# Block exchange through HBM with one store and one load of all partitions

## The chip, the cores and the metric

The kernel runs on one core of a Trainium2 chip. The metric is the device time of one execution in microseconds (us); lower is better. The core has a matrix engine (TensorE, PE in the profile), VectorE (DVE), ScalarE (ACT), GpSimd (POOL) and SyncE (SP), which here only issues DMA transfers. On-chip memory (SBUF) and the matrix engine's accumulators (PSUM) have 128 partitions; HBM is reached by DMA.

## The reference

A transformer block over 16 sequences of 256 tokens with 256 features: a layer norm with a shift from a conditioning vector, attention with 16 heads of 64 with normalised queries and keys, and a mixture of 8 experts in which every expert takes the 512 tokens with the largest gate. All of it is in 32-bit floating point.

```python
shift = silu(t) @ W_ada.T + b_ada
h = _ln(x, ln1_g, ln1_b) + shift
qkv = (h @ Wqkv.T).reshape(b, n, 3, H, HD)
q = _ln(qkv[:, :, 0].transpose(0, 2, 1, 3), qn_g, qn_b)
k = _ln(qkv[:, :, 1].transpose(0, 2, 1, 3), kn_g, kn_b)
v = qkv[:, :, 2].transpose(0, 2, 1, 3)
attn = softmax(einsum('bhnd,bhmd->bhnm', q, k) / sqrt(HD))
o = einsum('bhnm,bhmd->bhnd', attn, v)
x = x + o.transpose(0, 2, 1, 3).reshape(b, n, H * HD) @ Wout.T
tok = x.reshape(-1, d)
gate = softmax(tok @ Wgate.T)
vals, idx = top_k(gate.T, bs // E)
g = _ln(tok[idx], mlp_g, mlp_b)
y = gelu(g @ fc1s[e].T + b1s[e]) @ fc2s[e].T + b2s[e]     # for each expert e
out = tok.at[idx].add(y * vals)
```

## The kernel before

The program has a start-up (loads, centring of weights), an attention stage over the 16 sequences, a routing stage (which tokens go to which expert) and an expert stage of 16 jobs. Up to the first expert job the order of the instructions is written out by hand: every step is registered with `at(...)` (L1333 to L1517), and the list `PLACES` (L182 to L526) holds one number for each. `plan.order(PLACES)` (L1519) sorts by it, and the steps are issued in that order, so each engine and SP's DMA queue run their own steps strictly in this sequence. A step that must wait holds back all later ones of its engine.

**Queries and keys** (class `Group`). A group is 512 columns of the projection (8 heads of 64) for 128 tokens; groups 0 and 1 are the queries, 2 and 3 the keys, 4 and 5 the values, and t is the half of the sequence. TensorE multiplies (`matmul`, L688), ScalarE squares (L701), VectorE sums the squares of each head (`stats`, L705), GpSimd takes the power -1/2 (L711, L103), and VectorE multiplies each head by it (`scale`, L721). The means need no work there: the weight columns are centred once at the start, head by head (`center`, L604 and L605, eight calls, two for each group).

**The exchange.** The matrix engine needs features (and later keys) on the partitions, while they come out along the rows. Instead of transposing on TensorE, the kernel lets VectorE transpose blocks of 32x32 inside each band of 32 partitions (`turn`, L754 and L851). What is left is to bring block q of band k to band q. That goes through HBM. `away` (L761, L859) stores the 128 partitions of 4 KB each to a tile `blocks[k, m, q, 256]`, where k is the band, m the row in it and q the quarter, 1 KB each. The tile is made with five quarters, of which four are used, so the rows lie 5 KB apart. `back` (L773, L873) waits until the store has landed and issues four loads, one for each quarter q, of 32 partitions and four pieces of 1 KB each: row m of quarter q goes to partition 32q + m. Each sequence has four exchanges for queries and keys (tiles kb, kblocks, and qraw or kT) and eight for attention weights (pb, blocks, prT). All of them are issued on SP's queue, with the loads of x and the stores of tok and its norm. After the load, ScalarE applies gain and bias (`affine`, L781 for queries, L789 for keys).

The first and the last sequence (`DIRECT`, L171) do not use the exchange: TensorE transposes (L730, L881) and ScalarE copies out of PSUM (L742, L888).

**Attention** (class `Quad`, four heads). For a pair of heads (i), TensorE computes the scores into two PSUM tiles (`scores`, L813; there are four such tiles). VectorE takes the row maxima (L821), ScalarE the exponentials with their row sums (`exps`, L830), VectorE inverts the sums of both heads together (L837), GpSimd multiplies (L841), and VectorE turns the blocks (L851). The exchange brings the keys to the partitions, and TensorE multiplies with the values (`product`, L900), from where ScalarE copies to SBUF (L915). For the rows of the values to meet the right keys, the score columns are in the order (q, c, m): L806 reads the keys by quarter, so that column (q, c, m) is key 128c + 32q + m, and it lands on partition 32q + m.

**The rest of a sequence** (class `Tail`): the output projection (L926), the residual (L933), stores (L937, L947), and the gate's logits (L963).

Of the kernel before, what the change touches and what calls it, by code (L numbers as in the profile page):

```python
# [9 lines left out]
F32 = mybir.dt.float32  # L10
I32 = mybir.dt.int32
BF16 = mybir.dt.bfloat16
AF = mybir.ActivationFunctionType
ALU = mybir.AluOpType
AX = mybir.AxisListType
# [3 lines left out]
P = 128  # L19
B, N, D = 16, 256, 256  # L20
H, HD = 16, 64
# [5 lines left out]
TB = N // P  # L27
# [7 lines left out]
SQ = 32  # L35
QB = P // SQ
GW = 512
# [27 lines left out]
def kernel(  # L65
# [14 lines left out]
    nc = tc.nc  # L80

    const = ctx.enter_context(tc.tile_pool(name="const", bufs=1))
    dram = ctx.enter_context(tc.tile_pool(name="dram", bufs=1, space=DRAM))
# [87 lines left out]
    DIRECT = (0, B - 1)  # L171
# [356 lines left out]
    if True:  # L528
# [7 lines left out]
        wq = attw.tile([P, DC, 3 * H * HD], F32, name="wq")  # L536
        wo = attw.tile([P, HP, D], F32, name="wo")
        xs, hTs, qTs, kTs, vs, oTs = {}, {}, {}, {}, {}, {}
# [60 lines left out]

        def center(g, c):  # L600

            w3 = wq[:, c, bass.ts(g, GW)].rearrange("p (h d) -> p h d", d=HD)
            ws = stat.tile([P, 8], F32, tag="ws", bufs=2, name="ws")
            nc.vector.tensor_reduce(ws, w3, AX.X, ALU.add)  # L604
            nc.vector.scalar_tensor_tensor(  # L605
                w3, ws.unsqueeze(2).to_broadcast([P, 8, HD]), -1.0 / HD, w3, ALU.mult, ALU.add
            )

        class Norm:

# [21 lines left out]
        class First:  # L632
# [4 lines left out]
            def stats(self, t):  # L637
                self.norms[t] = Norm(xs[self.b][:, t, :], "l1")
# [34 lines left out]
        def plain(kT):  # L673
            return kT.rearrange("p g k t h m -> p (g k t h m)").rearrange("p (h n) -> p h n", n=N)

        class Group:
# [26 lines left out]
            def stats(self):  # L703
                self.ss = stat.tile([P, 2, 8], F32, tag="ss", name="ss")
                nc.vector.tensor_reduce(  # L705
                    self.ss[:, 0, :], self.sq.rearrange("p (h d) -> p h d", d=HD),
                    AX.X, ALU.add,
                )

            def power(self):  # L710
# [5 lines left out]
            def scale(self):  # L716
                engine, src = nc.gpsimd, self.qk
                if src is None:
                    self.qk = work.tile([P, GW], F32, tag="qk", bufs=3, name="qk")
                    engine, src = nc.vector, self.pm  # L720
                engine.tensor_tensor(  # L721
                    self.qk.rearrange("p (h d) -> p h d", d=HD),
                    src.rearrange("p (h d) -> p h d", d=HD),
                    self.ss[:, 1, :].unsqueeze(2).to_broadcast([P, 8, HD]), ALU.mult,
                )

            def transposes(self):
# [23 lines left out]
            def turn(self, kb):  # L751
                if self.t == 0:
                    kb.append(work.tile([P, QB, TB, HP // 2, SQ], F32, tag="pb", bufs=3, name="kb"))
                nc.vector.transpose(  # L754
                    kb[0][:, :, self.t],
                    self.qk.rearrange("p (h q d) -> p q h d", q=QB, d=SQ),
                )

            def away(self, kb):
                self.blocks = dram.tile([QB, SQ, QB + 1, N], F32, tag="blocks", bufs=4, name="kblocks")  # L760
                nc.sync.dma_start(  # L761
                    self.blocks[:, :, :QB].rearrange("k d q n -> (k d) (q n)"),
                    kb[0].rearrange("p q t h m -> p (q t h m)"),
                )

            def back(self):
                if self.g < 2:
                    self.raw = work.tile([P, QB, TB, HP // 2, SQ], F32, tag="qraw", bufs=2, name="qraw")
                else:
                    self.raw = self.keys()[:, self.g - 2]  # L770
                raw = self.raw.rearrange("p k t h m -> p k (t h m)")
                for q in range(QB):
                    nc.sync.dma_start(  # L773
                        raw[bass.ts(q, SQ)], self.blocks[:, :, q].rearrange("k d n -> d k n")
                    )

            def affine(self):
                if self.g < 2:
# [17 lines left out]
        class Quad:  # L796
# [5 lines left out]
            def scores(self, i):  # L802
                hp = 2 * self.d + i
                direct = self.b in DIRECT
                keys = plain(kTs[self.b]) if direct else (
                    kTs[self.b].rearrange("p g k t h m -> p g h (k t) m")  # L806
                )
                for j in range(2):
                    self.sc[i, j] = ps.tile([P, TB, N], F32, tag="sc", bufs=4, name="sc")
                for t in range(TB):  # L810
                    for j in range(2):
                        rows = slice(j * HD, (j + 1) * HD)
                        nc.tensor.matmul(  # L813
                            self.sc[i, j][:, t, :], qTs[self.b][rows, hp, bass.ts(t, P)],
                            keys[rows, hp] if direct else keys[rows, hp // 4, hp % 4],
                            start=True, stop=True,
                        )
# [7 lines left out]
            def exps(self, i, j):  # L825
                if i not in self.sums:
                    self.sums[i] = stat.tile([P, 2, 2, TB], F32, tag="sums", name="sums")
                self.pr[i, j] = work.tile([P, TB, N], F32, tag="pr", bufs=PRB, name="pr")
                for t in range(TB):
                    nc.scalar.activation(  # L830
                        self.pr[i, j][:, t, :], self.sc[i, j][:, t, :], AF.Exp,
                        bias=self.nmax[i, j][:, t : t + 1], scale=1.0,
                        accum_out=self.sums[i][:, 0, j, t : t + 1],
                    )
# [20 lines left out]

            def away(self, i):

                self.blocks[i] = dram.tile([QB, SQ, QB + 1, N], F32, tag="blocks", bufs=4, name="blocks")
                nc.sync.dma_start(  # L859
                    self.blocks[i][:, :, :QB].rearrange("k m q n -> (k m) (q n)"),  # L860
                    self.pb[i].rearrange("p q c h t n -> p (q c h t n)"),
                )

# [5 lines left out]
            def back(self, i):  # L869

                prT = self.turned(i).rearrange("p (k n) -> p k n", k=QB)
                for q in range(QB):
                    nc.sync.dma_start(  # L873
                        prT[bass.ts(q, SQ)], self.blocks[i][:, :, q].rearrange("k m n -> m k n")
                    )

            def transposes(self, i, j):
                self.pp[i, j] = ps.tile([P, TB, N], F32, tag="sc", bufs=4, name="pp")
# [465 lines left out]
        for g in range(4):  # L1344
            for c in range(DC):
                at(-200 + arrive[g], "DVE", 1.39, partial(center, g, c), [("wq", g)], [("wc", g)])
# [3 lines left out]
        for b in range(B):  # L1350
# [6 lines left out]
            a = First(b)  # L1357
# [9 lines left out]
            for (g, t), p in GROUP.items():  # L1367
                p += base
                a = Group(b, g, t)
                n = (b, g, t)  # L1370
                pm, sq, ss, qk, pq = (k + n for k in (("mm", 1), ("sq",), ("ss",), ("qk",), ("mm", 2)))
                need = [("hT", b)] + ([("wc", g)] if g < 4 else [("wq", g)])
                at(p, "PE", 1.73, a.matmul, need, [("pm",) + n], [pm, ("hT", b)], lag=0.22)
                if g < 4:
# [4 lines left out]
                    if b not in DIRECT:  # L1379
                        kb, blocks = ("pb", b, -1, g), ("blocks", b, -1, g)  # L1380
# [17 lines left out]
            for d in range(HP // 2):  # L1398
                a = Quad(b, d)
                p = base + d * QUAD  # L1400
                g = d // 2
                n = (b, d)
                po = ("po", 0) + n
                for i in range(2):
                    q = p + 3 * i
                    m = n + (i,)
                    sums, pb, prT, blocks = ("sums",) + m, ("pb",) + m, ("prT",) + m, ("blocks",) + m
# [20 lines left out]
            for t in range(TB):  # L1428
                a = Tail(b, t)
                p = base + TAIL[t]  # L1430
                n = (b, t)
# [55 lines left out]
        for n in range(2):  # L1487
            a = jobs[n]
            k = top + 10 + 20 * n
# [4 lines left out]
            for i in range(6):  # L1494
                name, took, by = {"D": ("DVE", 0.81, nc.vector), "P": ("POOL", 1.4, nc.gpsimd), "A": ("ACT", 3.5, nc.scalar)}[who[i]]
# [13 lines left out]
        k = top + 30  # L1509
# [36 lines left out]
        for k in range(1, len(jobs)):  # L1546
            a = jobs[k]
# [3 lines left out]
            for s in range(SLOTS):  # L1551
# [28 lines left out]
                else:  # L1580
                    i, q = divmod(s - FC, 4)
# [56 lines left out]
```

## Time and profile before

| what | us |
|---|---|
| median of three runs (lowest, highest) | 1090.54 (1088.64, 1091.8) |
| the profiled execution, its own time | 1091.3 |
| span of the profile | 1089.5 |
| attention stage in the profile | about 60 to 750 |
| routing stage | about 750 to 850 |
| expert stage | about 850 to the end |

The profile is of one execution, whose own time stands in the table; the span runs from its first to its last instruction. In a group line, the two shapes are output and input, then come the count, the busy time and the mean of one in nanoseconds, and behind the second bar the idle time in front of such instructions with what ended it. In a list of waits the numbers are the total in us, how often, and the longest. In the list of DMA issues they are the count, the KB of each and the median time in us from issue to landing. "x3: 174/175/391" is a count and the shortest, median and longest duration in nanoseconds.

### The profile page before, as it was taken

What the parts mean: (1) busy time and instruction counts of PE and PEld (TensorE: products, weight loads), DVE (VectorE), ACT (ScalarE), POOL (GpSimd) and SP (SyncE); (2) the same over time, 40 slices, a digit from 0 to 9 for tenths busy, and PEclk for the clock granted to TensorE, in tenths of its full rate; (3) what the DMA queues carried; (4) which work ended last, traced back from release to release, by engine and by line L of the source; (5) the groups of instructions that cost most, each with busy time, mean ns of one, the idle gap of its engine ahead of it and who ended that gap; (6) DMA issues with size and microseconds to landing.
All of it is one profiled execution on the core that took longest, in us unless ns stands there. A gap on an engine that the chain in (4) does not pass through costs nothing. (4 is left out here: it accounts for less than half of the span.)

```text
span 1089.5 us, 18716 instructions
## 1 busy us (share of the span) xinstructions
PE 1050.4 (96%) x5611; PEld 686.6 (63%) x5611; DVE 809.4 (74%) x2257; ACT 592.3 (54%) x1656; POOL 617.5 (57%) x997
## 2 busy tenths in 40 slices
PE   6999999999999999999999999999988999999996
PEld 4555646555454655555565555656667888888885
DVE  6658888889788797898888887885678588655440
ACT  1768666666566665675666656675612322332331
POOL 3676776778667686667757666665501333333332
PEclk9999999999999999999999999999999999999998
DMA  6025899999999999998999999985130556655661
GB/s 214 1 78 165 269 276 304 291 281 257 283 292 280 280 299 290 289 280 263 277 299 286 265 302 265 321 260 164 61 102 20 149 161 199 186 171 163 192 203 20
DMA packets 167700, 238.56 MB, mean 219 GB/s; under 512 B 17328, under 2 KB 139440, under 8 KB 167600
## 3 DMA queue, kind: packets, MB, share of 16 engines
q1 hardware_dynamic: 159680, 227.08, 69.9%
q0 software_dynamic: 6144, 8.39, 4.2%
q10 hardware_dynamic: 1776, 1.90, 0.5%
q8 instruction: 45, 0.74, 0.3%
q14 instruction: 55, 0.45, 0.1%
HBM read 136.64 MB, written 100.66 MB: 218 GB/s over the span
## 5 line engine op out<-in xcount | busy, mean ns | idle before, releaser
L688 PE MATMUL pm<-wq,hT 128*128 128x512 f32 x768 | 362.1, 607 | 10.1 <-DVE qk L721 3.9
L841 POOL TENSOR_SCALAR pr<-pr,sums 128x256 f32<-128x256 f32 x512 | 237.6, 485 | 102.6 <-DVE sums L837 95.0
L830 ACT ACTIVATE pr<-sc,nmax 128x256 f32<-128x256 f32 x512 | 237.7, 482 | 92.3 <-DVE nmax L821 75.2
L688 PEld LDWEIGHTS pm<-wq,hT 128*128 128x128 f32 x768 | 137.1, 191 | 165.3 <-issue 131.3
L103 POOL TENSOR_TENSOR ss<-ss,neghalf 128x8 f32<-128x8 f32 x128 | 211.2, 1650 | 10.7
L821 DVE TENSOR_REDUCE nmax<-sc 128x2 f32<-128x512 f32 x256 | 165.3, 672 | 19.4 <-PE sc L813 19.1
L851 DVE STREAM_TRANSPOSE pb<-pr 128x512 f32<-128x512 f32 x224 | 150.0, 689 | 15.9 <-POOL pr L841 9.4
L813 PE MATMUL sc<-kT,qT 64*128 64x256 f32 x1024 | 136.8, 396 | 1.0 <-ACT kT L789 0.6
L701 ACT ACTIVATE sq<-pm 128x512 f32<-128x512 f32 x128 | 76.4, 605 | 102.5 <-PE pm L688 100.5
L900 PE MATMUL po<-prT,v 128*64 128x256 f32 x1024 | 129.0, 387 | 1.3 <-DMA prT<-blocks 1.3
L813 PEld LDWEIGHTS sc<-kT,qT 64*128 64x128 f32 x1024 | 91.3, 186 | 50.3 <-issue 28.9
L1319 POOL DMA_INDIRECT out<-y,idx x32 | 51.3, 1604 | 120.6 <-DVE y L1313 66.0
L1286 PE MATMUL ph<-xT,w 128*128 128x256 f32 x512 | 117.8, 383 | 0.0
L1302 PE MATMUL py<-w,hid 128*128 128x256 f32 x512 | 116.3, 380 | 0.0
L926 PE MATMUL pw<-wo,oT 128*128 128x256 f32 x512 | 115.3, 382 | 0.0
L926 PEld LDWEIGHTS pw<-wo,oT 128*128 128x128 f32 x512 | 96.2, 190 | 20.9 <-issue 6.0
L830 ACT ACTIVATION_READ_ACCUMULATOR pr<-sc,nmax 128x1 f32 x512 | 109.2, 213 | 0.0
L900 PEld LDWEIGHTS po<-prT,v 128*64 128x64 f32 x1024 | 66.5, 136 | 66.0 <-issue 20.1
L705 DVE TENSOR_REDUCE ss<-sq 128x8 f32<-128x512 f32 x128 | 85.0, 669 | 28.8 <-ACT sq L701 28.3
L1293 ACT ACTIVATE hid<-ph,vec 128x256 f32<-128x256 f32 x128 | 60.4, 474 | 84.4 <-PE ph L1286 79.4
L1302 PEld LDWEIGHTS py<-w,hid 128*128 128x128 f32 x512 | 95.6, 190 | 12.8
L1286 PEld LDWEIGHTS ph<-xT,w 128*128 128x128 f32 x512 | 95.4, 190 | 12.8
(141 smaller groups left out, 1098.3 us busy)
## 6 DMA issues: line engine op xcount, KB each, us to landing
blocks<-pb SPq DMA_DIRECT2D x112, 512.0 KB, 4.7
prT<-blocks SPq DMA_DIRECT2D x448, 128.0 KB, 4.1
kblocks<-kb SPq DMA_DIRECT2D x56, 512.0 KB, 4.1
w<-in_fc2T SPq DMA_DIRECT2D x16, 1024.0 KB, 5.8
w<-in_fc1T SPq DMA_DIRECT2D x16, 1024.0 KB, 8.3
qraw<-kblocks SPq DMA_DIRECT2D x112, 128.0 KB, 4.0
kT<-kblocks SPq DMA_DIRECT2D x112, 128.0 KB, 4.1
out<-tok SPq DMA_DIRECT2D x32, 128.0 KB, 3.9
```

What stands on the lines that cost most here:

```text
L103: nc.gpsimd.tensor_tensor(dst, src, neghalf[:, : src.shape[1]], ALU.pow)
L688: nc.tensor.matmul(self.pm, hTs[self.b][:, c, bass.ts(self.t, P)], wq[:, c, bass.ts(self.g, GW)], start=(c == 0), stop=(c == DC - 1),)
L705: nc.vector.tensor_reduce(self.ss[:, 0, :], self.sq.rearrange("p (h d) -> p h d", d=HD), AX.X, ALU.add,)
L813: nc.tensor.matmul(self.sc[i, j][:, t, :], qTs[self.b][rows, hp, bass.ts(t, P)], keys[rows, hp] if direct else keys[rows, hp // 4, hp % 4] ...
L821: nc.vector.tensor_reduce(self.nmax[i, j], self.sc[i, j], AX.X, ALU.max, negate=True)
L830: nc.scalar.activation(self.pr[i, j][:, t, :], self.sc[i, j][:, t, :], AF.Exp, bias=self.nmax[i, j][:, t : t + 1], scale=1.0, accum_out=se ...
L841: nc.gpsimd.tensor_scalar(self.pr[i, j][:, t, :], self.pr[i, j][:, t, :], self.sums[i][:, 1, j, t : t + 1], 1.0, ALU.mult, ALU.mult,)
L851: nc.vector.transpose(self.pb[i][:, :, :, j].rearrange("p k c t n -> p t k c n"), self.pr[i, j].rearrange("p t (k c m) -> p t k c m", c=TB ...
L900: nc.tensor.matmul(self.po[j * HD : (j + 1) * HD, i, :], vs[self.b][:, c, bass.ts(4 * self.d + 2 * i + j, HD)], prT[:, j, c] if self.b in ...
L926: nc.tensor.matmul(self.pw, oTs[self.b][:, hp // 2, self.t, hp % 2, :], wo[:, hp, :], start=(hp == 0), stop=(hp == HP - 1),)
L1286: nc.tensor.matmul(self.ph[f], self.w1[:, c, bass.ts(f, P)], self.xT[:, c, :], start=(c == 0), stop=(c == DC - 1),)
L1302: nc.tensor.matmul(self.py[i], self.hid[:, f, bass.ts(i, P)], self.w2[:, f, :], start=(f == 0), stop=(f == FC - 1),)
```

## The change

One store and one load of all 128 partitions replace one store and four loads. The tile in HBM loses its fifth quarter, so rows lie 4 KB apart and the tile is contiguous; row m of quarter q now goes to partition 4m + q, which is the order in which the pieces of 1 KB lie in the tile.

Everything else follows from the new place. For queries and keys, partition 4m + q must hold feature 4m + q (counted over a pair of heads), so the columns of their weights are laid out on the host by quarter: column (q, e, d) of a group is feature 4d + q of head e. `center`, `stats` and `scale` follow with patterns over (q, e, d), where one head is four pieces of 16. In `center` the fused operation becomes a small multiplication and an addition, because the pattern has one dimension more. In the sequences of `DIRECT`, `scale` writes the columns back in the heads' own order, so neighbours are written four elements apart. For the attention weights, column (q, c, m) must be key 128c + 4m + q: the scores now come out in the keys' own order (the view of kT at L806 has t in front of k), and `exps` reads them from PSUM four elements apart and writes them in the order (q, c, m).

```diff
         def center(g, c):
-            w3 = wq[:, c, bass.ts(g, GW)].rearrange("p (h d) -> p h d", d=HD)
+            w3 = wq[:, c, bass.ts(g, GW)].rearrange("p (q e d) -> p q e d", q=QB, e=8)
             ws = stat.tile([P, 8], F32, tag="ws", bufs=2, name="ws")
-            nc.vector.tensor_reduce(ws, w3, AX.X, ALU.add)
-            nc.vector.scalar_tensor_tensor(
-                w3, ws.unsqueeze(2).to_broadcast([P, 8, HD]), -1.0 / HD, w3, ALU.mult, ALU.add
-            )
+            nc.vector.tensor_reduce(ws, w3.rearrange("p q e d -> p e q d"), AX.XY, ALU.add)
+            nc.vector.tensor_scalar_mul(ws, ws, -1.0 / HD)
+            nc.vector.tensor_tensor(w3, w3, by_head(ws), ALU.add)
+
+        def by_head(x):
+            return x.unsqueeze(1).unsqueeze(3).to_broadcast([P, QB, 8, HD // QB])
...
             def stats(self):
-                    self.ss[:, 0, :], self.sq.rearrange("p (h d) -> p h d", d=HD),
-                    AX.X, ALU.add,
+                    self.ss[:, 0, :], self.sq.rearrange("p (q e d) -> p e q d", q=QB, e=8),
+                    AX.XY, ALU.add,
...
             def scale(self):
+                if self.b in DIRECT:
+                    dst = self.qk.rearrange("p (e d q) -> p q e d", q=QB, e=8)
+                else:
+                    dst = self.qk.rearrange("p (q e d) -> p q e d", q=QB, e=8)
                 engine.tensor_tensor(
-                    self.qk.rearrange("p (h d) -> p h d", d=HD),
-                    src.rearrange("p (h d) -> p h d", d=HD),
-                    self.ss[:, 1, :].unsqueeze(2).to_broadcast([P, 8, HD]), ALU.mult,
+                    dst, src.rearrange("p (q e d) -> p q e d", q=QB, e=8),
+                    by_head(self.ss[:, 1, :]), ALU.mult,
                 )
...
             def turn(self, kb):
-                    self.qk.rearrange("p (h q d) -> p q h d", q=QB, d=SQ),
+                    self.qk.rearrange("p (q h d) -> p q h d", q=QB, d=SQ),
...
             def away(self, kb):
-                self.blocks = dram.tile([QB, SQ, QB + 1, N], F32, tag="blocks", bufs=4, name="kblocks")
+                self.blocks = dram.tile([QB, SQ, QB, N], F32, tag="blocks", bufs=4, name="kblocks")
                 nc.sync.dma_start(
-                    self.blocks[:, :, :QB].rearrange("k d q n -> (k d) (q n)"),
+                    self.blocks.rearrange("k d q n -> (k d) (q n)"),
...
             def back(self):
-                for q in range(QB):
-                    nc.sync.dma_start(
-                        raw[bass.ts(q, SQ)], self.blocks[:, :, q].rearrange("k d n -> d k n")
-                    )
+                nc.sync.dma_start(raw, self.blocks.rearrange("k d q n -> (d q) k n"))
...
             def scores(self, i):
-                    kTs[self.b].rearrange("p g k t h m -> p g h (k t) m")
+                    kTs[self.b].rearrange("p g k t h m -> p g h t k m")
...
             def exps(self, i, j):
                 for t in range(TB):
+                    dst, src = self.pr[i, j][:, t, :], self.sc[i, j][:, t, :]
+                    if not (self.b in DIRECT):
+                        dst = dst.rearrange("p (q c m) -> p q c m", q=QB, c=TB)
+                        src = src.rearrange("p (c m q) -> p q c m", q=QB, c=TB)
                     nc.scalar.activation(
-                        self.pr[i, j][:, t, :], self.sc[i, j][:, t, :], AF.Exp,
+                        dst, src, AF.Exp,
...
             def away(self, i):
-                self.blocks[i] = dram.tile([QB, SQ, QB + 1, N], F32, tag="blocks", bufs=4, name="blocks")
+                self.blocks[i] = dram.tile([QB, SQ, QB, N], F32, tag="blocks", bufs=4, name="blocks")
                 nc.sync.dma_start(
-                    self.blocks[i][:, :, :QB].rearrange("k m q n -> (k m) (q n)"),
+                    self.blocks[i].rearrange("k m q n -> (k m) (q n)"),
...
             def back(self, i):
-                for q in range(QB):
-                    nc.sync.dma_start(
-                        prT[bass.ts(q, SQ)], self.blocks[i][:, :, q].rearrange("k m n -> m k n")
-                    )
+                nc.sync.dma_start(prT, self.blocks[i].rearrange("k m q n -> (m q) k n"))
...
 def kernel(**inputs):
+    qk = a["Wqkv"][: 2 * H * HD].reshape(-1, 8, HD // 4, 4, D).transpose(0, 3, 1, 2, 4)
-        "wqkvT": a["Wqkv"].T,
+        "wqkvT": np.concatenate([qk.reshape(-1, D), a["Wqkv"][2 * H * HD :]]).T,
```

## The prediction

> **What bounds the kernel now.** I read the page first: what is full, and where.
>
> ```profile
> span 1089.5 us, 18716 instructions
> PE 1050.4 (96%) x5611; PEld 686.6 (63%) x5611; DVE 809.4 (74%) x2257; ACT 592.3 (54%) x1656; POOL 617.5 (57%) x997
> DMA  6025899999999999998999999985130556655661
> ```
>
> TensorE is busy 96% of the span, and the DMA line stands at 9 from slice 5 to slice 26: that is the attention stage, where the exchange runs. The second view gives busy time by stretch (PE, PEld, DVE, ACT, POOL with their counts, then clock, DMA share, GB/s).
>
> ```profile
> 100.00:750.00 650.00, 640.80 (x3114) 364.63 (x3112) 544.79 (x1087) 421.03 (x1252) 452.39 (x784) 1.00 0.97 280
> 0.00:60.00 60.00, 49.21 (x208) 29.06 (x209) 35.49 (x76) 28.80 (x67) 32.23 (x61) 0.97 0.29 98
> ```
>
> From 100 to 750 us TensorE is idle for 650 - 640.8 = 9.2 us, at the full clock; the change takes no work from it there, so 9.2 us is all that the stage can give. VectorE has 105 us of room, ScalarE 229, the DMA engines (share 0.97) next to none. The third view, TensorE's waits in this stretch, says who ends them.
>
> ```profile
> PE pm L688 <- ACT v L697: 1.9, 2, 1.2
> PE pg L952 <- ACT hT L659: 1.3, 1, 1.3
> PE po L900 <- DMA prT<-blocks: 1.3, 1, 1.3
> PE pm L688 <- DVE qk L721: 1.0, 3, 0.4
> PE pm L688 <- ACT hT L659: 0.8, 1, 0.8
> PE pl L963 <- ACT oT L915: 0.6, 1, 0.6
> PE sc L813 <- ACT kT L789: 0.6, 1, 0.6
> ```
>
> One is a transfer by name (po, 1.3). I followed three others back: sc (0.6) waited for the affine of kT, which had waited for its transfer; pl (0.6) and one pm (0.8) for ScalarE work queued behind the affine of qT, which had waited for qraw's transfer. So 3.3 of 9.2 us begin at the exchange.
>
> **Part 1: four loads become one.** In the stage 444 loads of prT and 208 of qraw and kT become 163. Each costs SP 430 ns (median of L873), so SP is freed for about 489 x 0.43 = 210 us; SP's queue holds the stores, x loads and tok stores behind them, which can only move forward.
>
> ```profile
> blocks<-pb SPq DMA_DIRECT2D x112, 512.0 KB, 4.7
> prT<-blocks SPq DMA_DIRECT2D x448, 128.0 KB, 4.1
> w<-in_fc2T SPq DMA_DIRECT2D x16, 1024.0 KB, 5.8
> out<-tok SPq DMA_DIRECT2D x32, 128.0 KB, 3.9
> ```
>
> Now the last of four lands 3 x 0.43 + 4.1 = 5.4 us after the first issue. The trace has no load of the new shape at 512 KB, but w<-in_fc2T has its pattern (128 partitions, rows of 1 KB one behind the other, steps of 128 KB) at twice the bytes: 5.8 us. Between that and 128 KB to 128 partitions (3.9): 3.9 + 1.9 x 384/896 = 4.7 us, with 3.9 and 5.8 as bounds. So 0.7 us an exchange before queueing. Queueing is the larger part: in the trace's packet records half of the stage's 1 KB packets take 46 ns and most others 60 to 100, while in the expert stage, whose loads reach all partitions, three of four take 46. At 46 ns for all, the 93,299 packets of 1 KB would take 268 us of 16 engines' time, not 385: share 0.97 falls to about 0.80, and stores land earlier too. What was late next: ScalarE waits 21.2 us for kT and qraw in this stage and VectorE 9.0 us for stores that free pb. I take the 3.3 us above as gone and half of the other 5.9, as they sit on those two queues: -6.2 us. Bounds: 0 (transfers no faster) and -9.2.
>
> **Part 2: the pitch of 4 KB.** It makes the block contiguous. Reads: the fc2T row has this layout and shows no loss. For stores of 4 KB rows there is no such row; nearest are the present stores (4.7) and tok's contiguous ones (3.9). I take no cost; a loss has no cover, since the share is 0.97.
> [...]
>
> **Part 3: exponentials read PSUM with a step of four.** 448 ACTIVATEs (L830, 483 ns, 256 elements) in the stage read with 16 bytes between neighbours. No row has ScalarE doing that. The nearest are these:
>
> ```profile
> L915 ACT COPY oT<-po x64: 562/587/686, 51.4 to 793.8; 128x512 f32<-128x512 f32 x64
> L697 ACT COPY v<-pm x64: 563/586/646, 29.6 to 757.4; 128x512 f32<-128x512 f32 x64
> L990 DVE TENSOR_TENSOR gates<-gates,smax x3: 174/175/391, 756.2 to 851.7; 128x16 f32<-128x16 f32 x2, 128x224 f32<-128x224 f32 x1
> L998 DVE TENSOR_TENSOR gate_of<-gates,smax x3: 185/186/765, 757.8 to 854.4; 128x16 f32<-128x16 f32 x2, 128x224 f32<-128x224 f32 x1
> ```
>
> L915 reads PSUM in reordered runs of 32 and costs what the plain copy L697 does: 0 per element. L998 is L990 with a step of 128 bytes on the written side: (186 - 175)/16 = 0.7 ns an element, or (765 - 391)/224 = 1.67 in the long one, during which GpSimd also ran. So 0 to 1.67 x 256 = 0.43 us an ACTIVATE. I take 0, from the same engine and memory as L915; ScalarE's 229 us of idle time would cover the first part of any price, and the second rival is what happens beyond.
> [...]
>
> **Part 4: the rest.** L705, L721 and the score matmuls keep their element counts with another order; L851, with five dimensions, takes 689 ns for 512 elements against L821's 672, so order alone costs nothing: 0, bounds 0 and +0.1 us each, under VectorE's 105 us of room. Centring: a 692 ns operation becomes one of 678 (as L721) and one on 128x8 of about 157 (as the copies of L969): +0.14 us, eight times. The first two lie in front of VectorE's 2.0 us wait for weights at 15.1 us; five precede the first scale at 23.4 us, for which TensorE waits 2.9 us: +0.7 us on the path. Sequences 0 and 15 write their scaled rows with a step of 16 bytes: by L998 0.36 to 0.86 us for 512 elements; two in that first chain count (23.4 and 26.8 us): +0.7 to +1.7, I take +0.7 (the undisturbed row). Sequence 15's are under VectorE's room.
>
> **Sum.** -6.2 + 0.7 + 0.7 = -4.8. The profiled execution took 1091.3 us (span 1089.5), 0.8 above the median of the runs. 1091.3 - 4.8 = **1086.5**; with the bounds of parts 1 and 4 from 1083.5 (-9.2 + 1.4) to 1093.7 (0 + 0.7 + 1.7).
>
> **Rivals.** *Hidden anyway*: the waits move to VectorE's and ScalarE's own order (5.9 of 9.2 us already end there), so only po's 1.3 us go: 1091.3 - 1.3 + 1.4 = 1091. For it: TensorE at 98.6% of the stage.
> *ScalarE pays for the step* (the slower side): at 0.7 ns an element an ACTIVATE is 0.18 us longer, the four in front of each of the 112 inversions (L837) 0.72 us. By the trace 54% of these start within 1 us of the last exponential, so VectorE slips by up to 112 x 0.54 x 0.72 = 44 us. Now TensorE idles 9.2 us beside 42 us of such waits (21.2 + 9.0 for transfers, 12.0 of VectorE for sums), about 0.22 each: +9.6, or 1096. It decides against the gain from 4.8/0.22 = 22 us of slip, 0.35 ns an element. Against it: L915.
> *The same at 1.67 ns*: ScalarE 421 + 448 x 0.43 = 614 of 650 us, 1.7 us per inversion, slip near 140 us against 105 of room: 35 + 0.22 x 105 = +58, about 1145.
> *The pitch costs*: with a share of 0.97, load packets 20% dearer add 77 us and the stage becomes DMA-bound, about 1140; decisive from +5%. Against it: fc2T.
>
> **How the numbers follow.** Forecast 0.42, hidden 0.15, step at 0.7 ns 0.30, at 1.67 ns 0.08, pitch 0.05. Over 0.3% (3.3 us) is what a measurement of this kernel can tell. Faster / same / slower: forecast 0.33/0.08/0.01, hidden 0.02/0.11/0.02, step 0.01/0.05/0.24, the last two slower: 0.36, 0.24, 0.40. The forecast's own range is 1083.5 to 1093.7; to hold 8 in 10 the range reaches over the step's case, 1082 to 1112, and leaves out the last two and the tails.
>
> **What would show it.** Right: L830 stays at 483 ns; DMA share near 0.80; the load lands in 4 to 5 us; the waits of ScalarE for kT and qraw vanish; TensorE idles 2 to 4 us from 100 to 750. Wrong: L830 above 570 ns with ScalarE waited for by L837; a DMA share that stays at 1; TensorE idle over 9 us; a start-up later by more than 3 us.

## The result and the profile after

| | before | after |
|---|---|---|
| median of four runs each, us (lowest, highest) | 1090.61 (1088.64, 1091.80) | 1081.45 (1080.74, 1082.01) |
| the profiled execution, its own time, us | 1091.3 | 1082.0 |
| span of the profile, us | 1089.5 | 1080.3 |

The ratio is 0.9917, with an interval from 0.990 to 0.9935: the change makes the kernel 0.83% faster. The forecast was 1086.5 us, with a range from 1082 to 1112. The sign was right, the gain was about twice the forecast, and the time lies just below the range.

The first lines of the page of the changed kernel, with the line of its DMA slices and that of its main queue:

```profile
span 1080.3 us, 17842 instructions
...
PE 1047.5 (97%) x5611; PEld 686.9 (64%) x5611; DVE 816.0 (76%) x2265; ACT 592.2 (55%) x1656; POOL 617.5 (57%) x997
...
DMA  6013889897887898987899797974030656665661
...
q1 hardware_dynamic: 151616, 227.05, 62.2%
```

VectorE has eight instructions more (one for each `center`), SP issues 504 loads fewer in the whole program (672 of prT, qraw and kT became 168), and the DMA slices, which stood at 9 with a few at 8 through the attention stage, now stand at 7 to 9. The view by stretch has the same columns as before (PE, PEld, DVE, ACT, POOL busy with their counts, then clock, DMA share, GB/s):

```profile
0.00:60.00 60.00, 46.73 (x184) 26.40 (x185) 38.52 (x83) 25.92 (x62) 28.99 (x56) 0.94 0.29 98
100.00:750.00 650.00, 649.99 (x3192) 373.64 (x3193) 555.68 (x1104) 432.08 (x1283) 458.67 (x791) 1.00 0.84 282
```

From 100 to 750 us TensorE is drawn as busy all the time (649.99 instead of 640.80 us), and its list of waits for this stretch is empty. The DMA share falls from 0.97 to 0.84 while GB/s stays (280 before, 282 now): the same bytes take less time. In the first 60 us TensorE does less than before (46.73 instead of 49.21 us): the start-up became later.

Where the time came from is best seen by following one and the same matmul through both traces. TensorE's 381st starts at 99.26 us before and at 102.56 after (+3.3), the 3581st at 762.92 and 753.13 (-9.8), and the last group at a difference of -9.4. So the start-up lost 3.3 us, the attention stage gained 13.1 and the rest gave back 0.4.

### The profile page after: what moved, and what is told of

It is laid out like the page before. It is cut to its first block, busy times and chain, and to the rows that moved or that the text cites. A ratio compares the mean times of both kernels' runs of the same rounds, so it can differ in the third digit from the quotient of the medians.

```text
span 1080.3 us, 17842 instructions
## 1 busy us (share of the span) xinstructions
PE 1047.5 (97%) x5611; PEld 686.9 (64%) x5611; DVE 816.0 (76%) x2265; ACT 592.2 (55%) x1656; POOL 617.5 (57%) x997
## 5 line engine op out<-in xcount | busy, mean ns | idle before, releaser
L727 DVE TENSOR_TENSOR qk<-pm,ss 128x512 f32<-128x512 f32 x128 | 93.6, 732 | 20.9 <-POOL ss L103 17.0
```

Source lines behind the costliest of these rows:

```text
L727: engine.tensor_tensor(dst, src.rearrange("p (q e d) -> p q e d", q=QB, e=8), by_head(self.ss[:, 1, :]), ALU.mult,)
```

## The experiments

Every variant was timed against the kernel before on its chip. Two numbers recur in what follows: the time from TensorE's 381st to its 3581st matmul in the profiled execution, called the stage (663.7 us before, 650.6 after), and the mean duration of the records of 1 KB packets from 100 to 750 us, with the share of them under 50 ns (66.0 ns and 49% before, 52.4 ns and 92% after). Both are worked out from the records of the trace.

### Which load is worth the gain

**Four loads of 32 neighbouring partitions, everything else as changed** (e1_4x32). A load takes eight rows of each band with all their quarters, so that row m of quarter q still goes to partition 4m + q:

```diff
-                nc.sync.dma_start(prT, self.blocks[i].rearrange("k m q n -> (m q) k n"))
+                for a in range(4):
+                    nc.sync.dma_start(
+                        prT[bass.ts(a, SQ)],
+                        self.blocks[i][:, bass.ts(a, SQ // QB)].rearrange("k m q n -> (m q) k n"),
+                    )
```

(Here and in the diffs below only the lines for the attention weights are shown; those for queries and keys, `raw`, are changed likewise.)

> New place, new pitch, but each load is cut into four of 32 partitions (band a of 32 partitions, 8 rows m, all four quarters). Theory (loads into 32 partitions collide, so their 1 KB packets take 60 to 100 ns instead of 46 and the DMA engines stand full): the packets, a DMA share near 0.97 and TensorE's idle time of 8 to 10 us in the stage from 100 to 750 us come back, beside the start-up's 3.3 us: 1091 to 1096 us. Rival A (it is the number of issues on SP): the same, 1091 to 1096, since there are four issues again. Rival B (it is that the tile is contiguous): stays at 1081 to 1083.

Measured: 1094.01 us, ratio 1.0013 (0.9999 to 1.0027). The whole gain is gone, as the theory and rival A had it; rival B, the contiguous tile, falls. The stage takes 665.4 us, the mean packet 67.1 ns. The stage's line in the view by stretch:

```profile
100.00:750.00 650.00, 639.82 (x3106) 364.79 (x3105) 547.48 (x1087) 421.63 (x1258) 449.84 (x781) 1.00 0.97 280
```

TensorE's and the DMA engines' numbers are those of the kernel before (640.80 us and 0.97). The new layout, the step in the exponentials and the pitch bring nothing without the new load.

**Four loads of 128 partitions, one for each band** (e2_4x128, repeated as a3_4x128):

```diff
-                nc.sync.dma_start(prT, self.blocks[i].rearrange("k m q n -> (m q) k n"))
+                for k in range(QB):
+                    nc.sync.dma_start(prT[:, k], self.blocks[i][k].rearrange("m q n -> (m q) n"))
```

> The changed kernel with four loads of all 128 partitions, one for each band k (128 KB each). Theory (collisions of loads into 32 partitions): packets stay near 46 ns, the share near 0.85, 1081 to 1083 us. Rival A (number of issues on SP): most of the gain is lost, 1088 to 1094. Rival B (contiguous tile): 1081 to 1083.

> The four loads of 128 partitions once more, to compare with one load and two loads, which stood at 0.9917 and 0.9914. If 0.4 us of SP for each load is worth the 3 us seen before, it repeats 0.994; if that was the chip, it comes out at 0.992.

Measured: 0.9943 (0.9926 to 0.9959) and, on another chip, 0.9937 (0.9921 to 0.9953). Its view by stretch in the first of the two:

```profile
100.00:750.00 650.00, 648.11 (x3174) 371.71 (x3172) 554.03 (x1101) 427.73 (x1276) 454.87 (x789) 1.00 0.85 282
```

The mean packet is 53.5 ns, the share 0.85, with as many loads as before. The stage takes 654.0 us in both profiles. The median of 1085.2 us lies between what the theory (1081 to 1083) and rival A (1088 to 1094) expected. So most of the gain needs no fewer loads, only loads that reach all partitions; the rest, some 3 us, repeats and goes with the number of loads.

**Two loads of 128 partitions, two bands each** (e6_2x128, beside the changed kernel once more, a2_again):

> The changed kernel once more, beside the three that follow. It should repeat its ratio to the kernel before, 0.992 (0.990 to 0.9935), TensorE busy for 650 of 650 us from 100 to 750 us and a DMA share of about 0.84 there.

> The changed kernel with two loads for an exchange, each of two bands to all 128 partitions. If the 3 us that four such loads lost against one are the time of issues on SP (0.4 us each), two loads lose about a third of it: ratio 0.993, TensorE busy about 649.5 from 100 to 750 us. If they were the difference of two chips, two loads equal one: the ratio of the run beside it within 0.001.

Measured: 0.9917 (0.9902 to 0.9933) for the changed kernel and 0.9914 (0.9899 to 0.9929) for two loads. Two loads are as good as one, where a third of the 3 us had been expected to be lost; the step from four to two is the one that counts (0.9940 to 0.9914, about 2.8 us; the intervals just overlap, the stages are 654.0 us twice against 651.2). In the trace SP's DMA issues from 100 to 750 us take 433 us with four, 280 with two, 166 with one.

**Two loads of 64 partitions, neighbours or every second one** (e9_2x64, again as a9_2x64, and e10_2x64step). These two differ in which 64 partitions a load writes and, with that, in which pieces of the block it reads (whole rows of 4 KB, or two of the four pieces of each row):

```diff
+                for h in range(2):
+                    nc.sync.dma_start(prT[bass.ts(h, 2 * SQ)],
+                        self.blocks[i][:, bass.ts(h, SQ // 2)].rearrange("k m q n -> (m q) k n"))
```
```diff
+                for h in range(2):
+                    nc.sync.dma_start(prT[bass.ds(h, 2 * SQ, step=2)],
+                        self.blocks[i].rearrange("k m (q h) n -> h (m q) k n", h=2)[h])
```

> The changed kernel with two loads of 64 neighbouring partitions each. SP issues as much as with two loads of 128 partitions (ratio 0.9914). If the gain comes from SP's time, it equals that, with a DMA share near 0.82 and packets at 46 ns. If it comes from the partitions that one load reaches, it lies between that and the four loads of 32 (1.0013): ratio 0.995 to 0.999, fewer packets at 46 ns (60 to 80% of them), share 0.87 to 0.94.

> Two loads of 64 neighbouring partitions once more, as the reference of the run beside it: 1.0036 (1.0018 to 1.0054) of the kernel before, 1 KB packets summing to about 400 us of 16 engines from 100 to 750 us, 0.61 us of SP for a load.

> The same with two loads of 64 partitions that take every second partition, so that each reaches over all 128. Number of loads, bytes, partitions for a load and order of issues stay. Theory (which partitions one load reaches sets what a packet costs): packets mostly at 46 ns, summing to about 310 us, share near 0.83, and a ratio of 0.992 to 0.995. Rival (the loss of the run beside it comes from SP, which spends 0.61 instead of 0.47 us on such a load, or from the count of 64): packets may be cheap, but the ratio stays at 1.000 or above.

Measured: neighbours 1.0036 (1.0018 to 1.0054) and 1.0050 (1.0031 to 1.0070); every second one, on the same chip as the latter, 0.9920 (0.9907 to 0.9932). The stage's lines of these two, neighbours first:

```profile
100.00:750.00 650.00, 639.49 (x3107) 364.22 (x3105) 546.81 (x1087) 421.77 (x1258) 449.65 (x781) 1.00 0.99 279
```
```profile
100.00:750.00 650.00, 647.97 (x3169) 371.34 (x3168) 554.24 (x1102) 428.97 (x1278) 456.95 (x789) 1.00 0.83 282
```

And what one such load costs SP (shortest, median, longest in ns, after the count), neighbours first:

```profile
L883 SPq DMA_DIRECT2D prT<-blocks x224: 573/608/1642, 100.1 to 750.2; - x112
```
```profile
L883 SPq DMA_DIRECT2D prT<-blocks x224: 579/608/1617, 100.5 to 739.1; - x112
```

SP pays the same 608 ns, the loads are as many and as large, and 1.3% lies between the two kernels. The expectation for neighbours, a ratio between those of 32 and of 128 partitions with 60 to 80% cheap packets, was missed: nothing is gained over 32. With neighbours 40% of the packets are under 50 ns (mean 69.5), with every second partition 94% (mean 52.3). This pair shows what the gain hangs on: a load of 64 neighbours is no better than one of 32, and a load of 64 that are spread over all is nearly as good as one of 128. That it is not the different reading in HBM, two further pairs of runs say: e3_pitch and e7_step4 read the same pieces at a pitch of 4 KB, the kernel before and e8_step4pad at 5 KB, and each pair differs in the load by the partitions alone, 32 neighbours or every fourth one. The mean packets are 68.8 and 50.9 ns, and 66.0 and 52.7 ns (at 277 and 265, and 280 and 266 GB/s).

**Four loads of 32 partitions, every fourth one** (e7_step4), and the same with the fifth quarter back in the tile (e8_step4pad):

```diff
-                nc.sync.dma_start(prT, self.blocks[i].rearrange("k m q n -> (m q) k n"))
+                for q in range(QB):
+                    nc.sync.dma_start(prT[bass.ds(q, SQ, step=QB)],
+                        self.blocks[i][:, :, q].rearrange("k m n -> m k n"))
```

> The changed kernel with four loads by quarter, each of 32 partitions, but of every fourth one (partitions q, q+4, ...), so that each load reaches over all 128. Theory (a load is slow when its 32 partitions are neighbours): it behaves as the four loads of 128 partitions did, ratio about 0.994, 1 KB packets mostly at 46 ns, DMA share about 0.85. Rival (a load is slow when it has only 32 partitions, or when it reads the block by quarters): it behaves as the four loads of 32 neighbouring partitions did, ratio about 1.001, fewer than half of the packets at 46 ns, share 0.97.

> The run before with the tile's fifth quarter back, a pitch of 5 KB. If the pitch of 4 KB costs by itself when the block is read by quarters (as it did with neighbouring partitions, +0.7%), this one is some 4 to 8 us faster than the run before. If it costs only where the loads are slow for their partitions, both are within 2 us.

Measured: 1.0378 (1.0350 to 1.0406) and 1.0344 (1.0323 to 1.0365). Both expectations for the time of the first were wrong. The packets are as cheap as the theory said (mean 50.9 ns, 89% under 50), yet the kernel loses 43 us. The stage's line, and the line of the load's issues:

```profile
100.00:750.00 650.00, 618.62 (x2919) 349.06 (x2918) 518.35 (x1034) 399.23 (x1182) 424.41 (x734) 0.98 0.77 265
```
```profile
L883 SPq DMA_DIRECT2D prT<-blocks x448: 577/602/1691, 99.2 to 789.1; - x150
```

The DMA engines are less busy than in any other variant (0.77), and TensorE waits 31 us. An issue takes 602 ns instead of 430, and all issues together 521 of the 650 us (411 before, 166 in the changed kernel); SP's own waits come to about 140 us (218 before). My reading is that SP's queue became the bound. It was not isolated, since no variant gave part of these loads to another queue, so why this kernel is slow stays open. Between the two pitches lie 3.7 us with intervals that overlap, so the pair leaves the price of the pitch under such loads open.

### What the other parts cost

**The pitch of 4 KB alone** (e3_pitch): the kernel before with the tile of four quarters, its four loads of 32 partitions kept.

```diff
-                self.blocks[i] = dram.tile([QB, SQ, QB + 1, N], F32, tag="blocks", bufs=4, name="blocks")
+                self.blocks[i] = dram.tile([QB, SQ, QB, N], F32, tag="blocks", bufs=4, name="blocks")
```

> The kernel before with the fifth quarter of the tile taken away and nothing else: rows 4 KB apart, four loads of 32 partitions. Theory (collisions): the pitch has no part in the gain, 1089 to 1093 us. Rival B (contiguous tile): 1081 to 1086. If rows of 1 KB that lie 4 KB apart are slow to read, the 1 KB packets lengthen, the share passes 1 and it takes over 1095.

Measured: 1099.39 us, ratio 1.0074 (1.0054 to 1.0093). The first expectation, that the pitch has no part, was wrong. The stage takes 672.9 us, 9.3 more than before. Its first waits of TensorE from 100 to 750 us (total, how often, longest):

```profile
PE sc L813 <- ACT kT L789: 4.0, 4, 2.6
PE po L900 <- DMA prT<-blocks: 2.1, 2, 1.7
```

Both are the exchange (0.6 and 1.3 us before). The mean packet went from 66.0 to 68.8 ns. So the fifth quarter was worth 8 us to the old loads. The changed kernel does without it; its stage has no wait of TensorE left that a padded tile could take away, but the changed kernel with a pitch of 5 KB was not run.

**The scaling in the first and last sequence** (e4_read, again as a4_read_again): it reads PSUM in the heads' own order, 512 bytes between neighbours, and writes neighbours side by side, instead of reading in runs and writing 16 bytes apart.

```diff
                 if self.b in DIRECT:
-                    dst = self.qk.rearrange("p (e d q) -> p q e d", q=QB, e=8)
+                    engine.tensor_tensor(
+                        self.qk.rearrange("p (e d q) -> p e d q", q=QB, e=8),
+                        src.rearrange("p (q e d) -> p e d q", q=QB, e=8),
+                        self.ss[:, 1, :].unsqueeze(2).unsqueeze(3)
+                        .to_broadcast([P, 8, HD // QB, QB]), ALU.mult,
+                    )
+                    return
```

> The changed kernel; in the first and last sequence the scaling runs in the heads' own order, so that it reads PSUM with a step of 512 bytes and writes without gaps, instead of reading without gaps and writing with a step of 16 bytes. If the price of 0.36 us an operation sits in the strided write, these operations fall from 1.05 to about 0.69 us, the start-up loses 1 to 2 us less and the time is 1079.5 to 1080.8. If a step costs on either side: 1081 to 1082.

> The changed kernel whose scaling in the first and the last sequence reads PSUM in steps and writes in order, once more beside the run that builds on it. It should repeat 0.9896 (0.9877 to 0.9915) of the kernel before.

Measured: 0.9896 (0.9877 to 0.9915) and 0.9889 (0.9869 to 0.9908). The scalings by shape, in the changed kernel and in the second run of this variant (count, busy time, mean ns of one):

```profile
L727 DVE TENSOR_TENSOR qk<-pm,ss 128x512 f32<-128x512 f32 x128 | 93.6, 732 | 20.9 <-POOL ss L103 17.0 <-PE pq L735 2.4
```
```profile
L731 DVE TENSOR_TENSOR qk<-pm,ss 128x512 f32<-128x512 f32 x112 | 75.9, 679 | 16.9 <-POOL ss L103 15.3
...
L724 DVE TENSOR_TENSOR qk<-pm,ss 128x512 f32<-128x512 f32 x16 | 10.9, 683 | 3.2 <-POOL ss L103 2.3 <-PE pq L740 0.8
```

A step on the reading side costs nothing (683 against 679 ns); on the writing side the sixteen cost 732 x 128 - 679 x 112 = 17,650 ns, 1.10 us each, 0.42 us more (the four of the start-up 1.04 to 1.07 us). This variant is 2 to 3 us faster than the changed kernel by its ratios and was the fastest of all, though the intervals of the two still touch.

**The order of VectorE's start-up** (e5_late): the variant above, with the centring of groups 1 and 3 moved behind the first four scalings.

```diff
-        ... 8, 9.39, 21.59, 15.62, 11.2, 13.11, 17.01, 18.4, ...
+        ... 8, 9.39, 27.1, 27.2, 11.2, 13.11, 28.9, 29.2, ...
```

> The run before, with the centring of groups 1 and 3 (four calls of 1.5 us on VectorE) moved behind the first four scalings, which now stand behind three of them. If VectorE's order sets the start-up, the first scaling comes about 3 us earlier (at 21 instead of 24 us) and the program ends 1.5 to 3 us earlier: 1076 to 1078, ratio 0.987 to 0.988. Rival: the matmuls of groups 1 and 3 then wait for their centred weights and give it all back, ratio as the run before within 0.001.

Measured: 0.9903 (0.9884 to 0.9922): no gain. The first scaling came at 22.3 instead of 24.2 us, but only as soon as GpSimd's power was ready, and the projection of groups 1 and 3 then waited for its weights. TensorE's waits of the first 60 us, the beginning of the list:

```profile
PE pm L690 <- DVE wq L606: 3.9, 4, 1.7
PE pm L690 <- ACT sq L703: 3.0, 2, 1.6
```

## Why the prediction was right and wrong

**Part 1, right in mechanism and too small in size.** This is the step that failed: the term was -6.2 us and the stage gave -13.1 (-13.2 in the second run of the changed kernel). Two things were mis-sized, the bound of the stage and the share of it that goes back to the exchange.

The bound "9.2 us is all that the stage can give" was wrong. I took it from TensorE's idle time, and that view undercounts. One of the waits in it, on the timeline of the kernel before (start, duration, instruction; in brackets the idle time in front):

```profile
278.42 1.45 PE L688 MATMUL pm<-wq,hT 128*128 128x512 f32 x3
281.18 0.44 PE L952 MATMUL pg<-ident,tok 128*128 128x128 f32 x2 [1.31 <-ACT hT L659]
```

Three matmuls are drawn with 1.45 us, that is two starts 0.43 us apart and 0.59 us for the last: in an unbroken row the next one starts 0.43 us after it (the median distance of two such matmuls from 100 to 750 us is 429 ns, before and after), so 0.16 us of this wait lie under "busy" (2.76 us from start to start, less 3 x 0.43 leaves 1.47, where the view shows 1.31). Measured from start to start, against the same matmuls in the changed kernel, the 21 visible waits of the stage come to 11.9 us instead of 9.2, and 22 other places, where the view shows no wait, to 1.0 us more. That is 12.9 of the 13.1 us gained.

And I counted 3.3 us plus half of the other 5.9 as the exchange's. The runs say all of it: with cheap packets and few loads no wait is left, whatever it was named after, and with four loads of 32 partitions they are back (e1_4x32). So the waits that ended on ScalarE for v, hT or tokT or on VectorE for qk were, as I read it, the same lateness passed on along in-order queues; I did not follow each of them back. The share of the "other" half was a guess where the question was whose queue they stood in. In numbers, the share cost 3.0 us (9.2 instead of 6.2) and the view 3.9 (13.1 instead of 9.2).

**What the packets did, as forecast.** I wrote 0.80 for the share and 46 ns for the packets; it became 0.84 (0.82 in the second run) and 92% under 50 ns. I had this from a row, the expert stage's loads; what the row did not tell was what made its packets cheap, and the pair of 64 neighbours (69.5 ns on average) and 64 spread partitions (52.3 ns) shows that it goes by which partitions a load reaches. The packets agree with this in every way of loading that was tried: 32 and 64 neighbours 66 to 70 ns on average, all 128 and the spread ones 50 to 54. Why neighbours cost more is shown by no run here.

**The load's landing, wrong and without harm.** I had 4.7 us against 5.4 for the last of four. The changed kernel's own trace gives no landing times for it, but that of the variant with the other scaling does (count, KB, median us from issue to landing):

```profile
blocks<-pb SPq DMA_DIRECT2D x112, 512.0 KB, 4.1
prT<-blocks SPq DMA_DIRECT2D x112, 512.0 KB, 5.3
kblocks<-kb SPq DMA_DIRECT2D x56, 512.0 KB, 3.2
```

One load of 512 KB lands 5.3 us after its issue, hardly earlier than the last of four did (within my bounds of 3.9 to 5.8). The stores land 0.6 and 0.9 us earlier (4.7 and 4.1 before). SP's freed time was right in direction, 411 - 166 = 245 us where I had 210. How it turns into the 2.8 us between four loads and two is not shown step by step; that it goes with the number of loads is. The waits that I had named as next went as forecast: ScalarE's for kT and qraw fell from 21.2 to 2.4 us in this stage, and VectorE's 9.0 us for stores are gone.

**Part 2, the pitch: 0 was not contradicted in this kernel, and the rival was nearer than its 0.05.** Alone, the pitch cost the old loads 8 us, with packets 4% dearer, a little under the +5% from which I had called it decisive, at a share of 0.98. In the changed kernel the share is 0.84 and TensorE has no wait in the stage, so a price of the pitch would find cover there; that is argued from the view, since the one load of 128 partitions was not run at 5 KB. Why the old loads lose at 4 KB against 5 KB (ratio 1.0074 in e3_pitch) is not shown.

**Part 3, the exponentials: right.** The line in the changed kernel, beside 483 ns before:

```profile
L836 ACT ACTIVATE pr<-sc,nmax 128x256 f32<-128x256 f32 x512 | 238.0, 484 | 89.8 <-DVE nmax L823 78.7 <-PE po L903 2.7 <-POOL ss L103 2.6
```

The line counts all 512; the 448 that read with the step take 485 ns on average, the same 448 before 483. The rival to which I gave 0.30 fell with this one number, and so did the one with 0.08 (whose slip "near 140 us" does not follow from my 54%, which gives 112 x 0.54 x 1.7 = 103). Neither ScalarE at 16 bytes between neighbours (485 against 483 ns) nor VectorE at 512 bytes (683 against 679 ns) paid for reading PSUM here. The row that I had for it (L915, the same engine and memory) was the better guide than L998, a write on another engine, and deserved more than it got.

**Part 4, the start-up: +1.4 forecast, +3.3 in the profile (+2.6 in the second run).** The centring costs 0.21 us a call from start to start instead of 0.14. The strided scalings were priced right (0.36, my lower row) but I counted two of them, and I put the clock at nothing. VectorE's and TensorE's lines around the four in the changed kernel:

```profile
23.94 1.05 DVE L727 TENSOR_TENSOR qk<-pm,ss 128x512 f32<-128x512 f32 x1
...
27.86 1.04 DVE L727 TENSOR_TENSOR qk<-pm,ss 128x512 f32<-128x512 f32 x1
...
30.19 1.04 DVE L727 TENSOR_TENSOR qk<-pm,ss 128x512 f32<-128x512 f32 x1
...
34.19 1.07 DVE L727 TENSOR_TENSOR qk<-pm,ss 128x512 f32<-128x512 f32 x1 [1.98 <-PE pq L735]
```
```profile
29.00 3.75 PE L690 MATMUL pm<-wq,hT 128*128 128x512 f32 x4 [1.46 <-ACT sq L703]
33.43 1.10 PE L735 MATMUL pq<-ident,qk 128*128 128x128 f32 x8 [0.68 <-ACT v L699]
35.41 1.07 PE L735 MATMUL pq<-ident,qk 128*128 128x128 f32 x8 [0.88 <-DVE qk L727]
```

The same four matmuls in e4_read, whose scalings write in order:

```profile
28.33 1.95 PE L690 MATMUL pm<-wq,hT 128*128 128x512 f32 x4 [1.64 <-ACT sq L703]
```

The fourth scaling comes 2.6 us later than before (31.55 us), and the second set of transposes waits for it. Beside e4_read, three of the four scalings stand on the chain: at the matmuls behind the first, the second and the fourth another 0.39, 0.28 and 0.38 us are lost. The third does not, since its transposes wait for the copy of the values (ACT v). The largest piece is another: the four matmuls in front of that copy take 3.75 instead of 1.95 us, and the granted clock from 29 to 33 us is 0.50 in the changed kernel and 1.00 in e4_read.

The start-up varies between profiles, and this clock varies with it. With this centring and these scalings the 381st matmul was 1.5 to 3.4 us later than in the profile before in eleven profiles, and all eleven have such a stretch of half clock among these matmuls (so has the profile before, with 0.66 from 24 to 29 us). With the scalings written in order it was 0.2 and 0.6 later, and 0.8 earlier in e3_pitch, whose start-up is the old one; these three have none there. So about two us go with the way the scalings write, but only some 1.1 of them are the scalings' own time. Whether the longer scalings bring the low clock, or it fell so by chance, is not shown.

**The sum.** -13.1 + 3.3 + 0.4 = -9.4 where I had -6.2 + 1.4 = -4.8. The time lies below the range because its lower end, 1082, leaned on the false bound of 9.2. The start-up's error went the other way and hid 1.9 us of part 1's.

**The signs and the rivals.** "Hidden anyway" would have shown as unchanged waits; the waits are gone. The step at 0.7 or 1.67 ns is excluded by 484 ns. The pitch is above. Of the signs of being right, TensorE's idle time of 2 to 4 us was missed (0.01 us) and the landing too (5.3 instead of 4 to 5 us); of the signs of being wrong one came, a start-up later by more than 3 us.

## What to carry to other kernels

Look at which partitions a DMA reaches before looking at how many loads there are: here 32 or 64 neighbours cost a quarter to a third more for each packet than 128 (66.0 and 69.5 ns against 52.4), and the same number spread over all did not (50.9 and 52.3 ns). But count the issues too: four spread loads of 32 had cheap packets (50.9 ns) and made the slowest kernel of all (1.0378). The idle time drawn in front of matmuls was less than the stage could give here (9.2 us, where 11.9 were lost from start to start at the same waits); measure from start to start, and follow one instruction through both traces to see where a gain is made and where it is given back. When a layout must be undone by a step, try the step on the side that reads PSUM first: here it cost nothing there (683 against 679 ns), and 0.42 us an operation on the side that writes SBUF (1.10 against 0.68).

## What the runs showed of the hardware that was not expected

- SP's median time to issue one load depended on its pattern: 374 ns for one load of all 128 partitions, 467 for each of two such, 430 for each of four, whether of 128 partitions or of 32 neighbours, but 602 to 608 for 64 partitions and for 32 spread ones.
- TensorE's granted clock fell to 0.50 for 3.4 or 6.8 us in the start-up of all profiles but one (a4_read_again), at different times; four 128x512 matmuls took 3.75 us in such a stretch and 1.95 outside.
- A pitch of 4 KB instead of 5 KB cost 0.74% (0.54 to 0.93) with four loads of 32 neighbouring partitions, in 1 KB pieces by quarter (e3_pitch).
- VectorE's write with 16 bytes between neighbours took 1.04 to 1.18 us for 512 elements a partition, against 0.68 in order; the same step read by ScalarE (485 against 483 ns), and one of 512 bytes read by VectorE (683 against 679 ns), took nothing.
